# Last layer of a four-layer 2D state-space network: written order on every engine, convolution on VectorE, last epilogue in four streams

## Chip, core and metric

The kernel is one program on one core of a Trainium2 chip. A core has five engines that run side by side, each with its own queue of instructions, which it takes strictly in order: PE (TensorE, matrix products, with its weight loads shown apart as PEld), DVE (VectorE), ACT (ScalarE), POOL (GpSimd), and SP, which here only starts DMA transfers. An instruction waits on semaphores for what other engines have to deliver; what stands behind it in the same queue waits with it. The metric is the device time of one execution in microseconds. Before the change it is 21146.67 us, the median of three runs (21117.39 to 21153.36).

## What is computed

Eight images of 48 x 48 pixels and 96 channels go through four layers of the same kind, each `x = x + ss2d(groupnorm(x))`. Cut to what matters, a layer is

```python
xz = gn(x) @ in_proj_w;  xc, z = split(xz)            # 192 channels each
xc = silu(depthwise_conv3x3(xc) + conv_b)
for each of 4 directions (rows, columns, and both reversed):
    dt, B, C = split(x_dbl(xc))                       # 16 states
    delta = softplus(dt @ dt_proj_w + dt_proj_b)
    y += scan(delta, A, B, C, xc) + xc * D            # over 2304 positions
y = layernorm(sum of directions) * silu(z)
out = x + y @ out_proj_w
```

In layers 0 to 2 the scan is the recurrence `h = exp(delta*A) * h + delta*u*B`, `y = sum over states of h*C`. Layer 3, the last, writes it differently: `decay = exp(cumsum(delta*A))`, `h = decay * cumsum(delta*u*B / (decay + 1e-12))`. As the decay is a product over all earlier positions it is zero in fp32 after a while, and from there on y holds only the skip term. The kernel uses this: in the last layer it scans only the first 192 positions (`EDGE`) of each direction, records for every channel whether the decay has vanished by then (`faded`), and would run the last layer again in full under a condition at the end if one had not. That second run is in the program but isn't executed.

## The kernel before

Images go in four pairs. 192 channels of two images are laid out as three tiles of 128 partitions: channels 0 to 127 of each image, and the remaining 64 of both together. For each layer and pair there are:

- the **prologue** (L276): group norm statistics on DVE and its scaling on ACT, the input projection on PE, copied by ACT into zero-padded images (`pad`), the 3x3 depthwise convolution (`convolve`, L291), and the projection that gives dt, B and C, written to DRAM. Before the change the convolution is on PE: for each tile and each chunk of ten rows nine matmuls with a diagonal weight add up in PSUM (L301), ACT takes the sum out with the bias (L309), and a silu over the whole tile follows. A silu needs another table in ACT and is bracketed by two table loads (L259, L260);
- the **scan**, in units. For the last layer `class Edge` makes 12 groups (three tiles, two orders, two directions) of four units; a unit is four of the 16 states over 192 positions. `prepare` (L563) makes delta by softplus for a group: a product on PE (L585), four steps on ACT and two on POOL, and the last on DVE (L607), from which L609 and L611 or L614 make `dl` and `du`; `sum_up` (L839) turns `dl` into a running sum. Per unit, `decay` is four exponentials (L880) on ACT, `spread` a logarithm and an exponential (L887, L888) and four small matmuls (L893), `scan` two products and four prefix sums on DVE (L898, L899, L901) and two products with C on POOL (L905, L906), and `add_up` four matmuls into `acc` (L913), issued four units later (`LAG`). `collect` adds `acc` to y (L935) and after the last group of a tile stores y to DRAM (L939);
- the **epilogue** (L942): y comes back in 16 chunks of three rows. Per chunk: layer norm over channels by centring matmuls (L956 to L962), copy and square on ACT (L996, L997), the mean of squares on PE again, Ln and Exp (L1006, L1007), a product on DVE (L1009), scale and shift on ACT (L1012), gates from PE (L1018, L1022) through silu, a second product on DVE (L1031), and the output matmuls (L1057 to L1059 in the last layer, L1036 to L1042 in the others), a copy by ACT (L1063) and a store.

Prologue and epilogue are Python generators that yield between small steps. `run` walks over all units of all layers and pairs, in each unit issues loads for units ahead, the scan, and steps of the epilogue of the pair before (`behind`) and of the prologue of the pair to come (`ahead`), which `side_step` picks by which has made less of its way. In layers 0 to 2 the written order is kept on every engine: `keep_order` chains the instructions between two marks, and the second mark is set at the first unit of the last layer. From there on the framework's own scheduler places the instructions of each engine, from what it expects of their times. So the order that the program has in the last layer isn't the order in the source. The last pair's epilogue has nothing beside it and is issued after everything else (L1221 and after).

PSUM is given out from three pools: `ps` with two banks for everything in prologue, epilogue and softplus (`bank()`), `b` with two double banks for the spread values, `acc` with one.

Of the kernel before, what the change touches and what calls it, by code (L numbers as in the profile page):

```python
# [102 lines left out]
def ss2d_layers_kernel(ctx: ExitStack, tc: tile.TileContext, x_in, consts, weights, out):  # L103
# [172 lines left out]
    def prologue(l, p, short=False, first=False):  # L276
# [14 lines left out]
        def convolve(pad, t):  # L291
# [3 lines left out]
            u[t] = upool.tile([P, L], F32, name=f"u_{l}_{p}_{t}", tag="u")  # L295
            for c0, m in CHUNKS:
# [266 lines left out]
    def prepare(c):  # L563
# [11 lines left out]
        for z in range(0, c.m, HALF):  # L575
            m = min(HALF, c.m - z)
            at = slice(z, z + m)

            ps = bank()
# [9 lines left out]
            yield  # L589
            nc.scalar.activation(v, v, AF.Identity, bias=ly.column(t, C_DTB + k))  # L590


            e = sm1.tile([P, HALF], F32, name="e", tag="e")[:, :m]
# [348 lines left out]
    def epilogue(l, p):  # L942
# [20 lines left out]

        def three():
            return bank()[:, : 3 * EM].rearrange("p (t m) -> p t m", t=3)
# [3 lines left out]
        def load(i):  # L969
            at = slice(ECHUNKS[i][0], sum(ECHUNKS[i]))  # L970
            x = sm2.tile([DM, 2, EM], F32, name="ex", tag="ex")
            nc.sync.dma_start(x, src[:, :, at].rearrange("b c m -> c b m"))
            y = sm2.tile([P, 3, EM], F32, name="ey", tag="ey")
            nc.sync.dma_start(y, yd[:, :, at].rearrange("t p m -> p t m"))
            loaded[i] = x, y

        load(0)
        for _ in range(3):
            yield
        for i, (c0, m) in enumerate(ECHUNKS):  # L980
            at = slice(c0, c0 + m)
            x, y = loaded.pop(i)
# [5 lines left out]
            xn = sm1.tile([DM, 2, EM], F32, name="exn", tag="exn")  # L988
# [6 lines left out]
            yc = sm1.tile([P, 3, EM], F32, name="eyc", tag="eyc")  # L995
# [30 lines left out]
            if i + 1 < len(ECHUNKS):  # L1026
                load(i + 1)
# [24 lines left out]
            ps = bank()[:q, : 4 * DM].rearrange("q (h b c) -> q h b c", h=2, b=2)  # L1052
# [16 lines left out]
        del state[l, p]  # L1069
# [44 lines left out]
    def run(pairs, short):  # L1114
# [22 lines left out]

        def get_ready(k):
# [7 lines left out]
            if k == 0:  # L1146
                todo[0][1].decay(todo[0][2])
# [6 lines left out]
            for i in range(k + DECAYS if k else 1, min(k + DECAYS + 1, len(todo))):  # L1154
                todo[i][1].decay(todo[i][2])
# [12 lines left out]
        for k, ((l, p, unit), c, n) in enumerate(todo):  # L1168
            at = pairs.index((l, p))
            following = pairs[at + 1] if at + 1 < len(pairs) else None  # L1170
            if l in short and unit == 0:
                mark()
# [14 lines left out]
            if n == max(0, per - 1 - DECAYS):  # L1187
                drain(coming)
            if n == 10 and coming_to + 1 < len(chunks):
                z = chunks[coming_to + 1]  # L1190
                if (z.l, z.p) == (l, p):
                    load_dt(z)
            busy = collected()
# [5 lines left out]
            def beside():  # L1199
                step(coming)  # L1200

                for _ in range(10 if l in short else 0 if ends else 1):
                    side_step(rest) or side_step(behind, ahead)

            ends = l not in short and k >= LAG and todo[k - LAG][2] == NS - 1
            if busy and l not in short:
# [124 lines left out]
```

## Time and profile before

| | us |
|---|---|
| median of 3 runs (lowest, highest) | 21146.67 (21117.39, 21153.36) |
| the profiled execution | 21131.57 |
| its span | 21129.7 |
| first scan product of the last layer (L898) starts | 19229.4 |
| last store of y (L939) starts | 20893.1 |
| stores of the third tile of y, pairs 0 to 3 | 19617.5, 20050.2, 20486.4, 20893.1 |
| busy in the whole span: PE, DVE, ACT, POOL | 18566.6, 18834.4, 13520.6, 17984.5 |

Times in the profile are microseconds from the start of the span unless ns is written. A group line gives the source line, engine, operation, `out<-in` with shapes, the number of instructions, busy time and mean duration, and after the bar the idle time of the engine just before them with what ended it. An fp32 matmul leaves two records. Busy time of an engine merges instructions that overlap, so that it can be less than the number of instructions times their mean. A wait for several things is put down to the one that came last.

### The profile page before, as it was taken

How to read it: one execution, taken by the hardware profiler on the slowest of the kernel's cores; microseconds unless marked ns; L12 is line 12 of the kernel's file. 1: busy time of each engine (PE TensorE's matmuls, PEld its weight loads, DVE VectorE, ACT ScalarE, POOL GpSimd, SP SyncE). 2: the span in 40 equal slices, each digit the busy share in tenths (PEclk: the TensorE clock that was granted, in tenths of full speed). 3: DMA queues.
4: the chain of work that ended last, by engine and by line, in shares of the span. 5: the costliest groups of instructions: out<-in, count | busy, mean ns of one | idle time of the engine just before them, and what ended most of it. 6: DMA issues, size and time to landing. Idle time of an engine off the chain costs nothing. (4 is left out here: it accounts for less than half of the span.)

```text
span 21129.7 us, 229163 instructions
## 1 busy us (share of the span) xinstructions
PE 18566.6 (88%) x64610; PEld 9118.1 (43%) x64610; DVE 18834.4 (89%) x15938; ACT 13520.6 (64%) x23969; POOL 17984.5 (85%) x11081
## 2 busy tenths in 40 slices
PE   8988998998998998998998988998998998988886
PEld 3333444443444443443443443443443443444555
DVE  6999999999999999999999999999999999997453
ACT  5555666666666665665666666665665666667776
POOL 5999898898899899898899989898999899896442
PEclk8999999999999999999999999999999999999887
DMA  4666666676676676676676666666666666674221
GB/s 137 195 193 193 188 196 194 190 196 195 190 200 195 192 201 195 190 204 191 191 204 195 191 194 195 190 197 190 191 197 193 190 196 195 189 194 123 79 74 51
DMA packets 1707632, 3832.96 MB, mean 181 GB/s; under 512 B 238448, under 2 KB 575216, under 8 KB 1693168
## 3 DMA queue, kind: packets, MB, share of 16 engines
q1 hardware_dynamic: 1706352, 3818.21, 61.9%
q8 instruction: 521, 8.54, 0.2%
q14 instruction: 759, 6.22, 0.1%
HBM read 3665.08 MB, written 152.27 MB: 181 GB/s over the span
## 5 line engine op out<-in xcount | busy, mean ns | idle before, releaser
L804 PE MATMUL acc<-cb,cst 128*128 128x384 f32 x27648 | 10706.0, 516 | 0.0
L768 POOL TENSOR_TENSOR cb<-cb,da 128x768 f32<-128x768 f32 x5184 | 9349.5, 1813 | 1393.2 <-DVE da L759 875.6
L804 PEld LDWEIGHTS acc<-cb,cst 128*128 128x128 f32 x27648 | 5003.6, 196 | 3957.4 <-issue 1498.2
L759 DVE TENSOR_TENSOR_SCAN da<-da,carry,b 128x768 f32<-128x768 f32 x3456 | 6268.3, 1814 | 220.9 <-ACT b L726 3.7
L755 DVE TENSOR_TENSOR b<-du,b 128x768 f32<-128x768 f32 x5184 | 4912.0, 948 | 685.4 <-PE b L743 678.8
L726 ACT ACTIVATE da<-dl,a 128x768 f32<-128x768 f32 x5184 | 4770.4, 926 | 95.6 <-POOL cb L768 60.4
L743 PE MATMUL b<-brow,pick 48*128 48x512 bf16 (+3 forms) x10368 | 2652.0, 337 | 1581.8 <-DVE da L759 1239.4
L726 ACT ACTIVATE b<-dl,a 128x768 f32<-128x768 f32 x1728 | 1560.3, 903 | 2960.1 <-DVE da L759 2817.4
L698 POOL TENSOR_TENSOR bb<-bb,du 128x768 f32<-128x768 f32 x1728 | 3131.3, 1812 | 183.4 <-DMA bb<-xd 142.8
L768 POOL TENSOR_TENSOR cb<-cb,bb 128x768 f32<-128x768 f32 x1728 | 3134.0, 1814 | 161.5 <-issue 56.8
L759 DVE TENSOR_TENSOR_SCAN da<-da,b 128x768 f32<-128x768 f32 x1728 | 3030.5, 1754 | 110.2 <-ACT b L726 2.4
L743 PEld LDWEIGHTS <-pick 48*128 48x128 bf16 (+1 forms) x10368 | 669.2, 97 | 4379.9 <-DVE da L759 2363.1
L759 DVE TENSOR_TENSOR_SCAN bb<-b,carry,bb 128x768 f32<-128x768 f32 x1152 | 2069.3, 1796 | 5.9 <-ACT b L726 2.2
L301 PE MATMUL ps<-pad,diag 128*128 128x480 f32 (+1 forms) x4320 | 2015.0, 565 | 15.1 <-DVE du L611 9.6
L650 ACT COPY carry<-da 128x1 f32<-128x1 f32 x3456 | 627.1, 181 | 1086.3 <-DVE da L759 1076.4
L590 ACT ACTIVATE ps<-ps,w 128x384 f32<-128x384 f32 (+1 forms) x912 | 497.1, 545 | 1027.5 <-PE ps L585 1022.9
L301 PEld LDWEIGHTS ps<-pad,diag 128*128 128x128 f32 x4320 | 804.2, 193 | 725.2 <-issue 330.3
L603 POOL TENSOR_TENSOR lg<-lg,w 128x384 f32<-128x384 f32 (+1 forms) x912 | 892.4, 978 | 195.0 <-ACT w L601 194.8
L585 PE MATMUL ps<-dts,w 6*128 6x384 f32 (+5 forms) x2432 | 821.2, 523 | 240.6 <-DVE du L611 99.9
L759 DVE TENSOR_TENSOR_SCAN bb<-b,bb 128x768 f32<-128x768 f32 x576 | 1000.1, 1736 | 16.3 <-POOL bb L698 9.8
L604 POOL TENSOR_TENSOR lg<-lg,e 128x384 f32<-128x384 f32 (+1 forms) x912 | 889.5, 975 | 71.2
L798 PE MATMUL acc<-y,cst 128*128 128x384 f32 x1008 | 619.1, 745 | 192.2 <-ACT y L819 127.2
(141 smaller groups left out, 17243.9 us busy)
## 6 DMA issues: line engine op xcount, KB each, us to landing
cb<-xd SPq DMA_DIRECT2D x4736, 384.0 KB
cb<-xd SPq DMA_DIRECT2D x4736, 192.0 KB
bb<-xd SPq DMA_DIRECT2D x1152, 384.0 KB
bb<-xd SPq DMA_DIRECT2D x1152, 192.0 KB
yd<-y SPq DMA_DIRECT2D x48, 1152.0 KB
ey<-yd SPq DMA_DIRECT2D x256, 216.0 KB
brow<-xb SPq DMA_DIRECT2D x576, 72.0 KB
ex<-xs SPq DMA_DIRECT2D x256, 108.0 KB
```

Source lines behind the costliest of these rows:

```text
L301: nc.tensor.matmul(ps[:, :m], ly.diag[:, int(t == 2), j, :], pad[:, r0 + dy : r0 + dy + nr, dx : dx + W], start=(j == 0), stop=(j == 8),)
L585: nc.tensor.matmul(o[:, :m], ly.dtw[q0 : q0 + r, k, chans], dts[q0 : q0 + r, at], start=True, stop=True,)
L603: nc.gpsimd.tensor_sub(lg, lg, w1)
L604: nc.gpsimd.tensor_add(lg, lg, e)
L650: nc.scalar.copy(*late_act.pop(0))
L698: nc.gpsimd.tensor_mul(b, b, self.du)
L726: nc.scalar.activation(da, self.dl, AF.Exp, scale=columns_of(self.l, self.t, self.ph, self.d, n))
L743: nc.tensor.matmul(b[:, z : z + zm], w, self.brow[:k, z : z + zm], start=True, stop=True)
L755: nc.vector.tensor_mul(b, self.du, b)
L759: nc.vector.tensor_tensor_scan(way(h), way(da), way(b), start, ALU.mult, ALU.add)
L768: nc.gpsimd.tensor_mul(c, c, h)
L804: nc.tensor.matmul(self.acc[:, a, : self.m // 2], ident, c[:, a, :], start=False, stop=(n == NS - 1 and not self.turns),)
```

## The change

Only the last layer's run is edited. Everything up to a few instructions before its first unit stands in the same order on every engine as before.

1. The second mark is set after the last epilogue, so that the written order is kept on every engine throughout the last layer too. Each of its units now issues: loads and decays for units ahead, its scan, the sums of the unit four back, and then five rounds of one step of softplus for the next group (in four of the five), one step of the prologue of the pair to come and one of the epilogue of the pair before. Before there were one softplus step and ten side steps a unit. Decays are issued two units ahead of their scan, counted from the unit that is under way, where they were three ahead; dt is loaded one group ahead of its softplus, where softplus itself used to load it.
2. In pairs 1 to 3 of the last layer the convolution is done by VectorE: nine instructions over a whole tile of 128 x 2304, one per tap, with the bias in the first. Pair 0 still has it on PE, in the layer before.
3. Softplus of the last layer moves its argument from PSUM into the free half of the tile `e` in SBUF, so that the bank is free after one read.
4. The last epilogue is split in four streams, each with every fourth chunk, stepped in turns and started three turns apart. Streams 2 and 3 take their PSUM tiles from the pool of the spread values. Streams 1 to 3 keep their four SBUF tiles in one buffer of another pool, and load a chunk when they begin it, not one ahead.

```diff
@@ convolve, at its start
+            if l == NLAYER - 1 and p > 0:
+                v = u[t].rearrange("p (r w) -> p r w", w=W)
+                for j in range(9):
+                    dy, dx = divmod(j, 3)
+                    z = pad[:, dy : dy + H, dx : dx + W]
+                    tap = ly.column(t, C_CONVW + j)
+                    if j == 0:
+                        nc.vector.tensor_scalar(
+                            v, z, tap, ly.column(t, C_CONVB), ALU.mult, ALU.add
+                        )
+                    else:
+                        nc.vector.scalar_tensor_tensor(v, z, tap, v, ALU.mult, ALU.add)
+                    yield
+                silu(u[t], u[t])
+                yield
+                return
@@ prepare
-            yield
-            nc.scalar.activation(v, v, AF.Identity, bias=ly.column(t, C_DTB + k))
-            e = sm1.tile([P, HALF], F32, name="e", tag="e")[:, :m]
+            e = sm1.tile([P, HALF], F32, name="e", tag="e")
+            if c.m == EDGE:
+                v = e[:, EDGE : 2 * EDGE]
+            else:
+                yield
+            nc.scalar.activation(v, ps[:, :m], AF.Identity, bias=ly.column(t, C_DTB + k))
+            e = e[:, :m]
@@ epilogue
-    def epilogue(l, p):
+    def epilogue(l, p, part=0, parts=1):
+        def own_bank():
+            return bank() if part < 2 else pb.tile([P, 2 * BANK], F32, name="b", tag="b")
...
         def load(i):
+            if part:
+                w = tmp.tile([P, 10 * EM], F32, name="ew", tag="tmp")
+                x, xn = (...)                      # x, exn, y, eyc all in w
...
-        load(0)
+        mine_of = range(part, len(ECHUNKS), parts)
+        load(part)
         for _ in range(3):
             yield
-        for i, (c0, m) in enumerate(ECHUNKS):
+        for i in mine_of:
+            c0, m = ECHUNKS[i]
+            if i not in loaded:
+                load(i)
...
-            if i + 1 < len(ECHUNKS):
-                load(i + 1)
+            if not part and i + parts < len(ECHUNKS):
+                load(i + parts)
@@ run, in each unit
-            if l in short and unit == 0:
-                mark()
...
-            if n == max(0, per - 1 - DECAYS):
+            if n == per - 1 - (1 if l in short else DECAYS):
                 drain(coming)
-            if n == 10 and coming_to + 1 < len(chunks):
+            if n == (0 if l in short else 10) and coming_to + 1 < len(chunks):
...
+            if l in short:
+                get_ready(k + 1)
+                c.scan(n)
+                collected()
+                catch_up()
+                if k >= LAG:
+                    (bl, bp, _), b, bn = todo[k - LAG]
+                    b.add_up(bn)
+                    if todo[k - LAG + 1][0][:2] != (bl, bp):
+                        done = bl, bp
+                if n == 0:
+                    while ahead.held and behind.held:
+                        side_step(behind)
+                for i in range(5):
+                    if i < 4:
+                        step(coming)
+                    side_step(ahead)
+                    side_step(behind)
+                continue
@@ run, at its end
-        drain(epilogue(*pairs[-1]))
+        streams = [epilogue(*pairs[-1], part, 4) for part in range(4)]
+        turn = 0
+        while streams:
+            streams = [g for i, g in enumerate(streams) if turn < 9 and turn < 3 * i or next(g, g) is not g]
+            turn += 1
+        mark()
```

## The prediction

> **What bounds the kernel now.** I read the page's slices first, then busy time by stretches, then the groups and waits of the last layer, then a timeline. Slices (busy tenths, 40 equal parts of the span):
>
> ```profile
> PE   8988998998998998998998988998998998988886
> ...
> DVE  6999999999999999999999999999999999997453
> ...
> PEclk8999999999999999999999999999999999999887
> ```
>
> VectorE (DVE) is full for 36 slices, the first three layers, and drops in the last four. The built order of every engine is unchanged until a few instructions before the last layer, so only the stretch from its first unit (19229 us) to the end counts: 1900 us of 21129.7. Busy time in its four pairs and its last epilogue (columns: stretch, length, busy us and records of PE, PE weight load, DVE, ACT, POOL, clock, DMA share, GB/s):
>
> ```profile
> 19229.00:19600.00 371.00, 328.87 (x1648) 218.93 (x1647) 206.97 (x367) 300.23 (x558) 177.84 (x119) 0.93 0.30 84
> 19600.00:20035.00 435.00, 366.38 (x1948) 252.71 (x1948) 225.36 (x393) 346.09 (x645) 191.44 (x135) 0.89 0.27 75
> 20035.00:20471.00 436.00, 365.81 (x1982) 252.73 (x1982) 224.77 (x392) 342.96 (x641) 191.43 (x134) 0.89 0.27 75
> 20471.00:20882.00 411.00, 273.40 (x1778) 223.93 (x1779) 220.25 (x386) 320.67 (x607) 185.20 (x121) 0.80 0.25 70
> 20893.00:21125.00 232.00, 153.65 (x1026) 130.80 (x1026) 19.52 (x34) 118.26 (x190) 0.00 (x0) 0.74 0.14 36
> ```
>
> In the first three pairs PE leads (84 to 89%) with ScalarE (ACT) close (79 to 81%); in the fourth, without a prologue, ACT leads (78%). In the last epilogue nothing does (PE 66%, ACT 51%): it is a chain. Its waits:
>
> ```profile
> DVE eyc L1009 <- ACT ps L1007: 171.8, 16, 16.3
> ACT eyc L996 <- PE ps L962: 50.5, 16, 22.5
> ...
> ACT eo L1063 <- PE ps L1059: 36.7, 16, 3.2
> ACT ps L1006 <- PE ps L962: 34.8, 16, 3.6
> ```
>
> Sixteen waits of each kind, one for each of 16 row chunks: 13.7 us a chunk (L1006 starts at 20936.40 and at 20950.23 on the chain). Groups of 19300 to 20850 (busy, mean ns, then idle before):
>
> ```profile
> L301 PE MATMUL ps<-pad,diag 128*128 128x480 f32 x632 | 265.7, 574 | 4.9 <-DVE eyc L1009 4.9
> L880 ACT ACTIVATE da<-dl,a 128x192 f32<-128x192 f32 x687 | 262.3, 443 | 26.0 <-DVE dl L839 25.8
> ...
> L899 DVE TENSOR_TENSOR b<-rq,b 128x768 f32<-128x768 f32 x171 | 162.6, 956 | 220.7 <-ACT rq L888 219.6
> ```
>
> The convolution is PE's largest group; VectorE waits for ACT. Last, a VectorE instruction with both inputs in SBUF, beside a GpSimd (POOL) product:
>
> ```profile
> 20095.12 1.81 POOL L906 TENSOR_TENSOR cb<-cb,rq 128x768 f32<-128x768 f32 x1 [1.38 <-DVE rq L901]
> 20095.21 2.13 DVE L839 TENSOR_TENSOR_SCAN dl<-ones,dl 128x192 f32<-128x192 f32 x1
> ```
>
> L839 has a median of 0.549 us; here it ends 0.4 us after POOL's product.
>
> [...] a pair of output passes takes 0.17 us between convolutions and 0.32 us in the last epilogue (clock 0.74). [...]
>
> **The change part by part.** Unit costs, from the groups and timelines. A unit (four states of 192 positions) is on ACT four decays, Ln and Exp, 4x0.443+0.925+0.834 = 3.53, back to back some 3.15 (six decays together take 2.18 us, not 2.66); DVE two products and four scans, 3.8; POOL 2x1.81 = 3.6; PE 0.65 for the spread and 1.7 for the sums. Softplus adds 2.25 of ACT to every fourth unit. One chunk of an epilogue is 118.26/16 = 7.4 of ACT, and the chain of 13.7.
>
> *Order.* Before, a scheduler places the instructions; now the written order holds on each engine: per unit the scan part, then five rounds of softplus, one prologue step and one epilogue step. Twelve epilogue steps make a chunk, so a chunk takes 2.4 units. Units 0 to 3 and five at the end have no side work: 9x4.3 = 39 (the last 16 units of before took 62 us, 3.9 each). With the epilogue alone: ACT 3.15+0.55+7.4x5/12 = 6.8. I walked the queues by hand through one cycle of 12 units (five chunks). Where a unit ends behind the silu, the next scan part hides the output passes; where it does not, as in the fifth unit, ACT is through its scan part at 3.15 and the silu at 6.2, whose result L1031 has multiplied by 5.6; the passes then last until 9.45 and the copy until 9.9, after 3.2 us of waiting. That happens in two chunks of five; a wait of 2.0 for the second mean (between L997 and L1006) in two others; shorter ones everywhere. Some 3.7 a chunk, 1.5 a unit: 8.3.
>
> *Convolution.* Removed per pair: 135 matmuls, 270 records of 0.41 us dense (18 take 7.4) = 111 us of PE, and 15 evictions of 0.64 = 9.6 of ACT. Added: 27 VectorE taps of 128x2304. The nearest row, L607, rises from 0.366 at 192 to 0.54 us at 384 elements, which gives 2.3; [...] I take 2.5[...]. That is 67 us a pair. Taps have two SBUF inputs, so each can stand behind a POOL product: 0 to 1.81 us. About two products fall in two units of taps: 3.6 a tile. Taps stand in two or three units per tile (in the second pair units 10 and 11, 18 to 20, 32 and 33). DVE then needs 2x3.8+22.5+3.6 = 34 for two units against 16.6; ACT can run ahead about one unit before its output copy and the tile's silu wait: net +13 a tile. Queued behind the taps are the epilogue's two products (L1009, L1031), and behind those ACT's next steps and the next scan.
>
> *Sum of a middle pair.* 17 units with the two images' prologue: ACT 17x6.8+20 copies of 0.5+6 for normalising+two silus of 4.65 = 141; waits 17x1.5 = 26; two convolutions 26: 193. Eleven with the epilogue alone: 91. Two with the third convolution: 43 (34 of DVE, 4 for softplus products and sums between the taps, the silu's 4.65 behind the last). Nine with projections: 8.3 and some 0.5 of copies each, 79. With 39: 445, against 435 and 436 before. The first pair's epilogue has 12 output records for 24: 20 less, 425, against 371. The last pair has no prologue: 39x8.4+39 = 367, against 411. Together 1682 against 1653: +29.
>
> *PE clock.* [...] the walk uses the slow 3.85 for outputs. Fast (2.0) would save up to 1.8 x16 a pair where ACT waits for it, some 12.
>
> *Softplus in SBUF* frees a PSUM buffer; its two products now can wait for POOL (0 to 1.8 each, twelve groups a pair). Nothing on ACT, as it is prepared a group ahead; without that cover, up to 20 a pair. *Loads.* Rows for C still go out three units ahead; earlier decay and dt moves only fill ACT's queue. The SP queue keeps written order, so a store that waits for L1063 holds the loads behind it, by less than a unit of the three: nothing. The 6.65 us store of y before the epilogue's first load stays in both.
>
> *Last epilogue.* Four streams share engines in turns. Bound: ACT 7.4 a chunk, PE 6.3 at full clock (outputs 2.0, the two means 1.6 each, gates 1.1), 153.65/16 = 9.6 at the clock of before. I take 8.4: streams 1 to 3 load without prefetch, 12 loads of 2.8 us landing, each issued about a turn early (0 to 34 together; I take 12). 16x8.4+7 for first store and load+14 until all streams run and drain+6 = 161, against 232: -71. Bounds: 145 and 205.
>
> Net +29-71 = -42: a span of 21088. The profiled execution took 21131.57, 15 under the median 21146.67 (runs spread 36); carried to the median: 21105. About 42 us (0.2%) is what a measurement can tell.
>
> **Rivals.** *Slower: the taps wait for POOL.* If every tap stands behind a product, 27x1.81 = 49 a pair instead of 11, three pairs +114: net +72, 21220. For it: L839's 2.13 and 3.65 for two; POOL has 3.6 a unit. Against: only two products a unit exist, unless waiting POOL and DVE alternate. It decides from 28 more a pair.
>
> *Faster: engines slip over units.* ACT stays 82% busy, as the walk has it without taps: busy (346 less 10 and some table loads, 332) gives 405 for each middle pair, by the same step about 360 and 375 for the first and last: 1545, a gain of 108. I keep 70 of it, since the taps' 13 a tile cannot all go; with -71 that is -141: 21005. For it: PE's 84 to 89% falls to some 60. Against: in-order waits of L1012 and L1063 behind taps.
>
> *No difference: the streams hold each other.* Two PSUM buffers for each two streams, and late loads: the last epilogue gains 25, not 71: net about 0, 21147.
>
> **How the numbers follow.** Forecast 0.45 (0.25 beyond -0.2%, 0.20 within; own range 21045 to 21165), faster rival 0.17, slower 0.30, no difference 0.08 (0.06 within, 0.02 slower). So faster 0.42, same 0.26, slower 0.32. The range leaves out half of the faster case and a third of the slower, 0.085 and 0.10: 21000 to 21235.
>
> **What would show it.** Right: taps near 2.5 us with some up to 4.3; pairs of 445, 367 last; the last epilogue near 161 with clock above 0.8; PE below 75% in the pairs. Wrong: middle pairs under 415 or over 470; taps of 4 us on average; a last epilogue above 200 with PE waiting for ey loads.

## The result, and the profile after

In what follows, before and after stand for the kernel before and the kernel after the change. After takes 21400.03 us (median of 4 runs, 21379.71 to 21419.24), before beside it 21150.01 (21117.39 to 21154.85). The ratio is 1.012, with a 95% interval of 1.0108 to 1.0132: about 250 us slower, outside the predicted range and beyond the slower rival as well. The slices of the page of after, in the same form as before:

```profile
PE   8988988988988988988988988988989988986666
...
DVE  6999999999999999999999999999999999996664
...
PEclk9999999999999999999999999999999999996777
```

The last layer now stands out on every engine at once: TensorE is at six tenths where it was at eight or nine, and its granted clock falls to seven tenths. VectorE rises from 4 or 5 tenths to 6. No engine is full, so the time went to waiting. Busy time in the four pairs and in the last epilogue (columns: stretch, its length, busy us and records of TensorE, its weight loads, VectorE, ScalarE, GpSimd, the clock, DMA share, GB/s):

```profile
19246.00:19757.00 511.00, 312.89 (x1500) 235.83 (x1500) 335.41 (x412) 339.29 (x626) 205.34 (x133) 0.70 0.23 65
19757.00:20276.00 519.00, 318.56 (x1712) 247.07 (x1712) 339.41 (x421) 338.00 (x625) 209.20 (x134) 0.70 0.23 63
20276.00:20795.00 519.00, 318.59 (x1712) 246.14 (x1712) 338.58 (x420) 337.25 (x622) 209.13 (x134) 0.71 0.23 63
20795.00:21204.00 409.00, 277.44 (x1638) 235.62 (x1638) 253.36 (x379) 296.23 (x554) 186.33 (x118) 0.75 0.24 70
21217.00:21417.00 200.00, 138.18 (x1026) 124.08 (x1026) 19.48 (x33) 116.55 (x192) 0.00 (x0) 0.79 0.16 43
```

In the second pair the three busiest engines have 339, 338 and 319 us of work in 519: 65% at most. ScalarE's work hardly moved (338 against 346). For the comparison of kernels I use one pair of marks throughout: a pair lasts from the first scan product of its first unit (L920, before L898) to the next pair's, the last pair to the last store of y, and the last epilogue from there to the end.

| us | pair 0 | pair 1 | pair 2 | pair 3 | four pairs | last epilogue |
|---|---|---|---|---|---|---|
| before | 413.1 | 437.4 | 435.7 | 377.5 | 1664 | 237 |
| after | 513.5 | 518.4 | 519.2 | 417.7 | 1969 | 200 |

The pairs lost 305 us, the epilogue gained 36. Layers 0 to 2 came 19 us later in this profiled execution (first L920 at 19248.1, against 19229.4); their order is unchanged, and the first scan product of the last layer starts anywhere from 19203 to 19248 us in the runs below. 305 - 36 + 19 is the 288 us between the two spans. So the pairs and the last epilogue are compared from here on, and not the totals alone.

VectorE's groups in the last layer of after (line, operation, `out<-in` and shapes, number, busy us and mean ns, idle before and its releaser):

```profile
L308 DVE SCALAR_TENSOR_TENSOR u<-pad,w,u 128x2304 f32<-128x2304 f32 x72 | 225.3, 3129 | 1.8
...
L861 DVE TENSOR_TENSOR_SCAN dl<-ones,dl 128x192 f32<-128x192 f32 x47 | 59.0, 1256 | 45.1 <-ACT dl L631 45.1
L629 DVE SCALAR_TENSOR_TENSOR e<-e,lg 128x192 f32<-128x192 f32 x47 | 52.9, 1125 | 81.8 <-POOL lg L626 81.8
L636 DVE TENSOR_TENSOR du<-e,u 128x192 f32<-128x192 f32 x24 | 43.1, 1798 | 0.7
L633 DVE TENSOR_TENSOR du<-e,u 128x192 f32<-128x192 f32 x23 | 39.5, 1717 | 0.5
```

A tap (L308) takes 3.13 us on the mean, with a smallest of 2.59 and a median of 2.62. With the first taps (L304, 2.38) the convolution is 247 us of VectorE, 82 a pair. The softplus's end grew too: L607 had 0.366 us before and is L629 with 1.125 now, and its two products went from 0.35 and 0.46 to 1.72 and 1.80. Together with the running sum (L861) these are 194.5 us, where the same four groups of before, from its first unit to its last store of y, are 73.5. The waits of after from 19200 us on (engine, its tile and line, who released it and where: us in total, times, longest):

```profile
POOL cb L928 <- DVE rq L923: 610.7, 130, 16.4
POOL lg L625 <- ACT w L623: 280.8, 47, 12.6
ACT e L612 <- PE ps L603: 277.3, 47, 22.5
DVE eyc L1053 <- ACT ps L1051: 265.1, 57, 18.3
...
DVE eyc L1075 <- ACT ps L259: 195.4, 44, 9.9
PE acc L935 <- DVE y L957: 193.5, 26, 20.3
PE ps L1102 <- DVE eyc L1075: 162.9, 33, 9.8
ACT eo L1107 <- PE ps L1103: 129.3, 38, 6.3
```

GpSimd, the least busy of the four, waits for VectorE and ScalarE; ScalarE waits for TensorE, VectorE for ScalarE, TensorE for VectorE. No engine is the one that all others wait for. A stretch of the timeline in the last pair shows one turn of this ring (start, length, instruction, idle time before it and who ended it):

```profile
20867.13 2.20 ACT L946 ACTIVATE y<-u,dsum 128x2304 f32<-128x2304 f32 x1
20869.36 0.35 DVE L957 TENSOR_TENSOR y<-y,acc 128x192 f32<-128x192 f32 x1 [6.65 <-ACT y L946]
...
20869.87 2.90 PE L935 MATMUL acc<-cb,cst 128*128 128x192 f32 x8 [3.34 <-DVE y L957]
...
20872.69 1.00 PE L603 MATMUL ps<-dts,w 6*128 6x192 f32 x2
...
20873.73 0.42 ACT L612 ACTIVATE e<-ps,w 128x192 f32<-128x192 f32 x1 [4.40 <-PE ps L603]
```

ScalarE writes the skip term of y; VectorE has stood 6.65 us for it, to collect a finished group; only then may TensorE put the next group's first sum (L935) into the one accumulator; behind these sums stands the softplus's product L603, for which ScalarE has meanwhile waited 4.40 us. My walk had none of these steps: it didn't ask when `acc` comes free.

### The profile page after: what moved, and what is told of

The parts are those of the page before. It is cut to its first block, busy times and chain, and to the rows that moved or that the text cites. A ratio compares the mean times of both kernels' runs of the same rounds, so it can differ in the third digit from the quotient of the medians.

```text
span 21417.4 us, 227251 instructions
## 1 busy us (share of the span) xinstructions
PE 18469.9 (86%) x63800; PEld 9133.3 (43%) x63800; DVE 19214.0 (90%) x16019; ACT 13506.1 (63%) x23910; POOL 18044.0 (84%) x11081
## 4 chain that ended last, share of the span: by engine, by line
DVE 43%; PE 27%; ACT 12%; issue 10%; DMA 6%; POOL 2%; SPq 1%; DVEq 0%; POOLq 0%; ACTq 0%
DVE da L781 21%; DVE b L777 12%; PE acc L826 12%; DVE bb L781 4%; DMA cb<-xd 3%; PE b L765 3%; PE ps L318 3%; PE acc L820 2%; PE ps L603 2%; ACT da L748 2%; ACT b L748 2%; DVE ps L629 1%; DMA brow<-xb 1%; POOL cb L790 1%; ACT y L841 1%
## 5 line engine op out<-in xcount | busy, mean ns | idle before, releaser
L318 PE MATMUL ps<-pad,diag 128*128 128x480 f32 (+1 forms) x3510 | 1695.7, 569 | 9.6 <-DVE du L633 9.6
L612 ACT ACTIVATE ps<-ps,w 128x384 f32<-128x384 f32 x864 | 478.4, 554 | 1024.0 <-PE ps L603 1019.6
L928 POOL TENSOR_TENSOR cb<-cb,rq 128x768 f32<-128x768 f32 x192 | 364.0, 1896 | 810.4 <-DVE rq L923 610.7
L603 PE MATMUL ps<-dts,w 6*128 6x384 f32 (+5 forms) x2432 | 831.3, 529 | 217.6 <-DVE du L633 79.9
L318 PEld LDWEIGHTS ps<-pad,diag 128*128 128x128 f32 x3510 | 654.4, 194 | 572.8 <-issue 207.0
```

The costliest lines, as they stand in the source:

```text
L318: nc.tensor.matmul(ps[:, :m], ly.diag[:, int(t == 2), j, :], pad[:, r0 + dy : r0 + dy + nr, dx : dx + W], start=(j == 0), stop=(j == 8),)
L603: nc.tensor.matmul(o[:, :m], ly.dtw[q0 : q0 + r, k, chans], dts[q0 : q0 + r, at], start=True, stop=True,)
```

## The experiments

I began with three causes that the profile suggests, each as a theory of its own: **A**, the single accumulator (the ring above); **B**, the lock between VectorE and GpSimd over the softplus in SBUF (a VectorE instruction with two operands in SBUF and a GpSimd product hold each other up: L839 in the forecast's timeline takes 2.13 us for a median of 0.549, and in after GpSimd's products, with a median of 1.81 us, last up to 4.13 beside taps); **C**, the taps. The rival to all three is that the order itself costs. In what follows, before's median in the same comparison lies between 21127 and 21141 us.

**1. Two accumulators.**

```diff
-                self.acc = pacc.tile([P, 2 * BANK], F32, name="acc", tag="acc")
+                if "acc" not in place:
+                    place["acc"] = pacc.tile([P, 2 * BANK], F32, name="acc", tag="acc")
+                self.acc = place["acc"][:, BANK * (groups.index((self.t, self.ph, self.d)) % 2) :]
```

> The kernel after, but the groups of the last layer add up by turns in two accumulators, the two banks of the same PSUM tile, so that a group's first sum no longer waits until VectorE has collected the group before. Nothing else is changed. Theory A, the accumulator holds the loop (first sum L935 waits for the collecting L957, the softplus matmul stands behind it on TensorE, and ScalarE waits for that): 100 to 180 us less than after, so 21220 to 21300, and the waits of L935 for VectorE, 193.5 us over 26 in after, gone. Theory B, the lock between VectorE and GpSimd over the softplus sets the period: within 30 us of after. Theory C, the convolution's taps on VectorE set it: within 30 us of after.

Measured 21390.56 us (1.0127, 1.011 to 1.0144), pairs of 514, 518, 519 and 418. But the first sum still waits for the collecting, 193.4 us over 26, as in after. The edit did not take the wait away, so it tests nothing. That the two banks of one tile count as one thing for the synchronisation is my guess at the reason; the new wait in the next experiment, between two banks of the same tile, fits it.

**2. The softplus's argument in a free PSUM bank.**

```diff
-                v = e[:, EDGE : 2 * EDGE]
+                v = place["acc"][:, BANK : BANK + EDGE] if "acc" in place else e[:, EDGE : 2 * EDGE]
```

> The kernel after, but the argument of the softplus goes to the unused second bank of the accumulator instead of SBUF, for all groups but the first of the layer, so that VectorE's three operations of it read one operand from PSUM and two no longer come from SBUF. Theory B, the lock with GpSimd: VectorE's sum of the three operations and the running sum falls from 194.5 us to about 75 in the 48 groups, and the time by 90 to 130 us, to 21270 to 21310. Theory A, the accumulator: 20 to 40 us less at most, since VectorE only comes a little earlier to the collecting. Theory C: the same 20 to 40.

Measured 21397.24 us (1.0132, 1.0115 to 1.0149). The lock is gone from the operations that now have an operand in PSUM, as VectorE's groups show:

```profile
L629 DVE SCALAR_TENSOR_TENSOR acc<-acc,lg 128x192 f32<-128x192 f32 x46 | 16.5, 360 | 188.5 <-PE acc L937 132.2 <-POOL lg L626 23.8 <-ACT da L902 23.0
...
L636 DVE TENSOR_TENSOR du<-acc,u 128x192 f32<-128x192 f32 x24 | 11.3, 473 | 31.9 <-ACT dl L631 31.9
L633 DVE TENSOR_TENSOR du<-acc,u 128x192 f32<-128x192 f32 x22 | 7.8, 355 | 22.8 <-ACT dl L631 22.8
```

0.36 us in the place of 1.125, and the sum of all four groups falls from 194.5 to 89 us. The time stands still, since a new wait of 132 us for TensorE's sums into the same tile came in. So B's mechanism is shown, but not its price: the run took one wait and brought another.

**3. The convolution on TensorE, order kept.** In `convolve` the taps make way for nine matmuls and an eviction a step:

```diff
-                        nc.vector.scalar_tensor_tensor(v, z, tap, v, ALU.mult, ALU.add)
...
+                    for j in range(9):
+                        nc.tensor.matmul(ps[:, :m], ly.diag[:, int(t == 2), j, :], ...)
+                    yield True
```

> The kernel after, but the convolution of the last layer's later images runs on TensorE again, nine matmuls and one eviction a step, in the place of the taps in the order. Theory C, the taps: VectorE loses 247 us, the three pairs with a prologue lose 60 to 90 each, so 21130 to 21220. Theory A: the taps are 82 us of a pair on an engine that the collecting waits for, 20 to 40 a pair come back, 21280 to 21340. Theory B: the same as A. The granted clock of TensorE in those pairs, 0.70 in after, should rise above 0.80 in each case.

Measured 21474.36 us (1.0163, 1.0146 to 1.018), with pairs of 540, 547, 553 and 413: the first three slower than after by some 30 each. The loss stays without the taps, so C falls as its cause. Of two kernels with the order kept, the one with taps is the better; what the taps alone cost isn't shown, as the matmuls that take their place stand in the order too. The clock of TensorE rose to 0.81 in the second pair, as all three theories said, with 404 us of work in 547.

**4. The same kernel, placed by the scheduler.**

```diff
             if l in short:
+                if unit == 0:
+                    mark()
                 get_ready(k + 1)
```

> The kernel after, but the last layer's instructions are placed by the scheduler as before, from the same written order, taps, softplus and streams. If the fixed order itself is what costs (each queue stands behind the first instruction that waits): 150 to 250 us less than after, 21150 to 21250. If the places of the data cost (the softplus in SBUF, the one accumulator, the taps on VectorE): less than 60 us less, 21340 or more.

Measured 20963.88 us, a ratio of 0.9921 (0.9905 to 0.9938): 436 us less than after, and faster than before. Taps, softplus, one accumulator, units' turns and streams are all still there. Its stretches, first the four pairs, then the last epilogue:

```profile
19247.00:19648.00 401.00, 291.10 (x1524) 220.97 (x1522) 302.83 (x414) 328.01 (x623) 222.79 (x134) 0.78 0.30 86
19648.00:20053.00 405.00, 290.04 (x1716) 226.41 (x1716) 305.34 (x419) 333.13 (x631) 225.66 (x135) 0.79 0.28 80
20053.00:20469.00 416.00, 299.42 (x1713) 232.59 (x1712) 302.44 (x414) 332.64 (x629) 224.43 (x131) 0.76 0.27 77
20469.00:20832.00 363.00, 252.13 (x1638) 210.61 (x1638) 230.80 (x383) 297.16 (x570) 189.28 (x120) 0.82 0.27 76
20832.00:20966.00 134.00, 108.45 (x1026) 94.97 (x1026) 19.38 (x33) 110.10 (x184) 0.00 (x0) 0.95 0.22 59
```

The same work with the same engine time (ScalarE 333 us in the second pair, 338 in after) takes 405 us where it took 519: ScalarE is now 82% busy. The pairs cost 1584 us, 385 less than in after, and the last epilogue 134, 66 less. The wait of the first sum for the collecting does not come up among the longest any more. So the loss lies in the order that was kept. Each engine has one sequence in either kernel: TensorE's 1712 records, VectorE's 419 and ScalarE's 622 of after's second pair come back line for line in its third, and so do the 1982, 392 and 641 of before, where the scheduler placed them. The scheduler's queues are simply other ones than the source's. "Kept" below always means this one written order. No run tries another written order, so whether a better one would do as well as the scheduler's stays open.

**5. One engine's order kept.** These runs keep the order on TensorE alone, ScalarE alone, VectorE alone:

```diff
-    def keep_order(a, b):
+    def keep_order(a, b, engines=ENGINES):
...
     keep_order(*marks[:2])
+    keep_order(*marks[1:3], ENGINES[:1])     # or [2:3], or [1:2]
```

> The kernel after, with the written order of the last layer kept on TensorE alone; the scheduler places the other four engines' instructions. With all five kept it takes 21400, with none 20964. If the first sum of a group, which waits for the accumulator with the softplus matmul behind it, is what stops the loop, TensorE's order alone brings most of the 436 us: 21250 or more. If it is another engine's order, less than 100 of them: below 21065.

> The same with the order kept on ScalarE alone. ScalarE carries most of a unit's other steps (decay, spread, softplus, silu, evictions), so a wait at its head holds everything: if that is the cause, 21200 or more. If TensorE's order is the cause: below 21065. In the last epilogue the streams' written turns should show on ScalarE first: 160 to 200 us there against 134 in the scheduled one.

> The same with the order kept on VectorE alone, where the taps, the softplus and the collecting stand between the scans. If a tap or a softplus step at the head of the queue holds the scans: 21150 or more. If the order of TensorE or ScalarE is the cause: below 21065.

Measured 20976.51 us (0.9924, 0.9907 to 0.994), 20997.71 (0.9931, 0.9914 to 0.9947) and 20969.62 (0.9925, 0.9908 to 0.9941). The expectations speak of the whole layer, but a mark is set at the first unit of every pair, so the order was kept in the first pair only. There the pair takes 427.8, 457.9 and 431.4 us, against 401.0 with none kept and 513.5 with all five: TensorE's order costs 27 us, ScalarE's 57, VectorE's 30. None alone brings the 113. These prices are rough: the second pair, where nothing is kept in these runs or in the scheduled kernel, takes 405 to 417 us.

**6. The streams alone in the kernel before**, with `epilogue` and its streams from after, and everything placed by the scheduler:

```diff
-        drain(epilogue(*pairs[-1]))
+        streams = [epilogue(*pairs[-1], part, 4) for part in range(4)]
...
```

> The kernel before, with only the last epilogue in four streams, all placed by the scheduler. The scheduled kernel with all the edits has an epilogue of 134 us, before has 236. If the streams carry the gain of the scheduled kernel: 21010 to 21050, 80 to 110 less than before. If they owe it to the rest (the taps and the softplus in SBUF, 80 us over the four pairs): the same epilogue gain, and the pairs as before, so that these two add up to the 163 us between the scheduled kernel and before. If they help only together with the rest: less than 50.

Measured 21029.69 us, 0.9951 (0.9934 to 0.9968). The last epilogue is 136 us, against 237, and the pairs are as before (417, 437, 435, 382). So of the 163 us by which the scheduled kernel beats before, the streams bring 100.

**7. Collecting ahead of the scan**, the order kept, as another test of A:

```diff
-                c.scan(n)
                 collected()
+                c.scan(n)
```

> The kernel after, all five orders kept, but in each unit of the last layer the collecting of the finished group stands ahead of the unit's scan on VectorE and not behind it. Theory A, the accumulator holds the loop: the 193.5 us over 26 that the first sum waits for VectorE fall below 60, and the time by 60 to 150, to 21250 to 21340. Theory D, the orders together cost because each unit's work lies unevenly over the engines and every unit lasts as long as its busiest: the wait moves to another line, the time within 40 us of after.

Measured 21339.18 us (1.0094, 1.0077 to 1.0111), 61 less than after, which is A's smallest gain; A's other sign, a wait below 60 us, did not come. The pairs are 500, 504, 504 and 410. Its waits:

```profile
ACT e L612 <- PE ps L603: 199.5, 40, 18.7
...
PE acc L935 <- DVE y L957: 138.9, 19, 16.5
...
DVE y L957 <- ACT y L946: 109.9, 12, 12.9
```

The first sum still waits 139 us, because VectorE itself now waits longer for ScalarE's skip term (110 us, 54 in after). A is a part of the loss, some 15 us a pair by this way of shortening it. It is not the whole.

**8. One engine freed.** The order of the last layer kept on four engines, or on three:

```diff
+    keep_order(marks[1], marks[5], ENGINES[:2] + ENGINES[3:])   # ScalarE free
+    keep_order(marks[1], marks[5], ENGINES[:1] + ENGINES[2:])   # VectorE free
+    keep_order(marks[1], marks[5], ENGINES[1:])                 # TensorE free
+    keep_order(marks[1], marks[5], ENGINES[:3])                 # GpSimd and DMA queue free
+    keep_order(marks[1], marks[5], ENGINES[:2])                 # TensorE and VectorE kept
```

> The kernel after, with the written order kept on four engines in the last layer's four pairs and all of ScalarE's instructions placed by the scheduler (the last epilogue is placed by it on all engines; the order of layers 0 to 2 is kept as ever). Each engine's order alone, kept in the first pair only, cost 27 us (TensorE), 57 (ScalarE) and 30 (VectorE) there, where all five cost 113. If these add up engine by engine, the pairs lose 45 to 55 us each against the fully scheduled 401, 405, 416, and ScalarE's share is gone: 21100 to 21170 in all. If ScalarE's order is the one that couples the others, the loss is gone with it: below 21040. If the other four hold each other without it: above 21200.

> The kernel after, with the order of the last layer kept on four engines and VectorE placed by the scheduler. In after VectorE stands at the head of its queue for epilogue steps (L1053 266 us, L1075 195 us) and for the collecting while scans that could run stand behind. If VectorE's fixed order is what couples the engines, the pairs fall from 518 to 400 to 440: 20980 to 21130. If any four hold each other as with ScalarE free (505): 21250 or more.

> The same with TensorE free: the sums, with the softplus matmul and the prologue's and epilogue's matmuls behind them, may pass one another. If TensorE's fixed order couples the engines: pairs of 400 to 440, 20980 to 21130. If any four hold each other: pairs of about 500, 21250 or more.

> The order kept on TensorE, VectorE and ScalarE together, GpSimd and the DMA queue placed by the scheduler. If the three compute engines suffice to hold each other: pairs of 490 to 520, 21300 or more. If GpSimd's products standing behind its softplus steps (L625 waits 281 us for ScalarE in after) or the loads in the DMA queue are part of the hold: pairs below 470, below 21220.

> The order of the last layer kept on TensorE and VectorE together, the other three engines placed by the scheduler. Fully scheduled, a pair takes 401 to 416; in the first pair, TensorE's order alone gave 428 and VectorE's alone 431; with three engines kept (TensorE, VectorE, ScalarE) 507 to 512. If the cost comes as soon as two engines cannot slip against each other: pairs of 470 or more, 21150 or more. If their costs only add: pairs of 440 to 465, about 21100.

In all five the order was kept in the last epilogue as well. The expectation of the first says otherwise, and is wrong in that.

| order kept on | median us | ratio to before, interval | pair 0 | pair 1 | pair 2 | pair 3 | last epilogue |
|---|---|---|---|---|---|---|---|
| all five (after) | 21400.03 | 1.0108 to 1.0132 | 513.5 | 518.4 | 519.2 | 417.7 | 200 |
| all but ScalarE | 21311.48 | 1.007 to 1.0103 | 500.9 | 504.6 | 504.9 | 387.4 | 193 |
| all but VectorE | 21329.27 | 1.0074 to 1.0108 | 487.7 | 493.7 | 494.5 | 420.5 | 200 |
| all but TensorE | 21234.15 | 1.003 to 1.0064 | 490.7 | 494.3 | 491.6 | 383.2 | 150 |
| TensorE, VectorE, ScalarE | 21327.49 | 1.0077 to 1.011 | 507.1 | 511.6 | 511.9 | 417.8 | 167 |
| TensorE, VectorE | 21187.56 | 1.0013 to 1.0034 | 475.1 | 476.1 | 474.7 | 365.8 | 171 |
| none | 20963.88 | 0.9905 to 0.9938 | 401.0 | 404.5 | 415.9 | 362.8 | 134 |

Read by their expectations, the rest hold each other whichever of TensorE, VectorE and ScalarE is freed (with TensorE free the total, 21234, falls just short of the 21250 named, since the last epilogue gains 50 there), three are enough, and two cost somewhat more than the sum of their single prices: 74 us in the first pair for 27 + 30, which is 17 more with some 12 us of scatter in such prices. Freeing one of the three gives a middle pair back 14 to 28 of some 110 us, and freeing GpSimd with the DMA queue 7. So in the pairs with a prologue no engine's order is the cause by itself; what costs there is that the written order stands on several engines at once. The last pair, without prologue and taps, is different: of the 55 us that it loses, 34 come back with TensorE free and 30 with ScalarE free, none with VectorE free, and with TensorE and VectorE alone kept it loses 3 (366 against 363).

How several fixed queues lose can be read from the units. I cut each engine's queue at its own instruction of each unit (first scan product, second step of the reciprocal on ScalarE, first spread matmul, first C product), took of the four busy times in each unit the largest, and added these over the 48 units of the second pair. If all engines went through the units in step, none working into its neighbour unit, and nothing else was waited for, a pair would last about that long:

| second pair | busiest engine's work | sum of units' largest | measured |
|---|---|---|---|
| after | 342 | 455 | 518.4 |
| TensorE, VectorE, ScalarE kept | 337 | 453 | 511.6 |
| all but ScalarE kept | 350 | 498 | 504.6 |
| all but VectorE kept | 337 | 445 | 493.7 |
| all but TensorE kept | 340 | 496 | 494.3 |
| TensorE, VectorE kept | 344 | 468 | 476.1 |
| none kept | 337 | 465 | 404.5 |

The scheduled kernel is 60 us below that sum, so its engines run ahead of each other over unit bounds. After is 64 us above: in the sum its engines gain nothing by slipping past each other, and waits between them come on top. With two or more orders kept the second pair is at most 2 us below its sum; with one kept, the first pair is below it by 5 (TensorE), 17 (ScalarE) and 66 (VectorE). The sum alone does not order the kernels, since the scheduled one has a larger sum than after, and it depends on the cuts: with TensorE's cut one unit later after has 465. It is a reading of how the time goes, and no proof. The chain of waits gives an example. This piece of after's chain, from its second pair (start, length, instruction), goes from ScalarE's queue into VectorE's at an epilogue step, and then through three taps that stand there back to back, 9.3 us in all, and a product of the epilogue (L1075); the next unit's scan (L920) stands behind them.

```profile
19865.42 0.52 ACT ps L1051
19865.94 0.02 issue
19865.97 0.60 DVE eyc L1053
19866.57 2.54 DVE u L308
19869.11 0.03 issue
19869.13 4.05 DVE u L308
19873.18 0.02 issue
19873.21 2.62 DVE u L308
19875.83 0.51 DVE eyc L1075
19876.34 0.88 DVE b L920
```

**9. What the parts are worth under the scheduler.** From the scheduled kernel: the convolution back on TensorE; the softplus's argument back in its own bank; both; the softplus back and only one of three tiles with taps.

```diff
-            if l == NLAYER - 1 and p > 0:                 # (removed: convolution on TensorE)
...
-                v = e[:, EDGE : 2 * EDGE]
+            yield
+            nc.scalar.activation(v, v, AF.Identity, bias=ly.column(t, C_DTB + k))
...
+            if l == NLAYER - 1 and p > 0 and t == 1:      # (in the last: one tile)
```

> The scheduled kernel with all edits (20964), but the later images' convolutions on TensorE again. If the taps carry the gain of its pairs over before (80 us in four pairs; TensorE's convolution is 75 of a pair's 438 us in before's chain of work): 30 to 90 us more, 20995 to 21055, and the granted clock of TensorE in the pairs changes with it. If they don't: within 20 us.

> The scheduled kernel with all edits (20964), but the softplus's argument stays in its PSUM bank as before. VectorE's operations of it are short again (0.37 and 0.35 us against 1.13 and 1.72), but each softplus holds one of the two banks over six steps. If the bank is dearer: 20 to 60 us more than 20964. If the lock with GpSimd is dearer: 20 to 60 us less, 20905 to 20945.

> The scheduled kernel with both the softplus in its PSUM bank and the convolutions on TensorE, so that of the change only the turns of the units and the four streams stand. Undone alone, the softplus gave 24 us and the convolution 17. If they add up: 20910 to 20935. If each pays because it takes load off VectorE where the other one put it: 20930 to 20950. Against before with the streams alone (21030) the difference is what the turns are worth under the scheduler: 80 to 120 us.

> The scheduled kernel with the softplus in its PSUM bank and only one of a pair's three convolutions (channel tile 1) as taps on VectorE. In the pair's 405 us TensorE is busy for 394 with all three convolutions on it, ScalarE for 341 and VectorE for 227; one convolution moved takes some 27 us from TensorE and gives VectorE about 27. If TensorE's load is what sets a pair there: pairs of 380 to 395, 20840 to 20890. If the chain through all engines does: within 15 of the 20918 with none moved.

| scheduled | median us | ratio to before, interval | pairs 0 to 3 |
|---|---|---|---|
| all edits | 20963.88 | 0.9905 to 0.9938 | 401, 405, 416, 363 |
| convolution on TensorE | 20947.00 | 0.9896 to 0.9929 | 396, 406, 406, 366 |
| softplus in PSUM | 20939.71 | 0.9892 to 0.9925 | 402, 416, 408, 355 |
| both | 20918.03 | 0.9885 to 0.9918 | 405, 405, 406, 355 |
| softplus in PSUM, one tile with taps | 20911.82 | 0.9875 to 0.9908 | 399, 401, 401, 352 |

The intervals overlap: taps and softplus in SBUF make no difference that these runs can tell. With both undone the median is 46 us lower; but of the 52 us between the two profiled executions 39 lie ahead of the last layer, and the pairs and the last epilogue differ by 13. The turns of the units do make one. With both undone only the streams and the turns (with the decays and loads that go with them) are left of the change, and 0.9901 against 0.9951 for the streams alone is 0.5%, with intervals apart; the pairs take 1572 us against 1671. One tile moved takes a pair from 405 to 401 us, not to 380 to 395, so TensorE's load alone is not the bound of the scheduled pairs either. (Its 394 us in the expectation were too many: the stretch of that pair has 364 us of TensorE's work.) The last kernel takes 1.1% less than before and some 2.3% less than after.

## Why the prediction was wrong

**Order.** This is the step that failed. It priced the written order at 1.5 us of waits a unit, from one cycle of queues walked by hand, and only the epilogue's own waits were in that. The 445 us of a middle pair, some 56 of them such waits (37 units of 1.5), became 518 to 519, the first pair's 425 became 511 to 514, the last pair's 367 became 409 to 418. (The 371 and 411 that I set against the first and last came from stretches that end ahead of the pair and begin ahead of it; by the marks used here before has 413 and 378, and 1664 in all four for my 1653, so that this changes little in the sum.) The last pair has neither prologue nor taps, so some 55 us are lost there by the order with the epilogue alone: with no order kept it takes 363, close to my 367. The two middle pairs lie 114 and 103 above their scheduled times, 405 and 416. The walk left out three handoffs that the trace shows: the accumulator (193.5 us of waiting), the softplus's product behind it (277.3), and the softplus's last steps on VectorE behind GpSimd. Easing one at a time gave 3 to 61 us, and in both runs another wait grew (132 us for TensorE's sums, 110 for the skip term). Outside the convolutions I also took a unit's length from ScalarE's queue; in the second pair ScalarE has the most work in 15 of the 48 units, VectorE in 18, TensorE in 13. These largest alone come to 455, so that my 445 is near them and has hardly anything for the waits between the engines on top.

**Convolution.** The mechanism was right and the size nearly so. 2.5 us a tap was the forecast: L607's two lengths gave 2.3, and no trace had shown the rest. 2.6 is the plain length: the smallest tap is 2.591 us and the median 2.619. Waiting behind GpSimd was put at 11 us a pair (3.6 a tile); 72 taps x (3.129 - 2.6) over three pairs are 12.7. The whole is 82 us a pair for 67 + 11. With the order kept, the kernel without the taps was even the slower one.

**Softplus in SBUF.** I had put it at nothing for ScalarE, and at up to 20 us a pair if being prepared a group ahead did not cover it. Its operations on VectorE take 121 us more in the layer (194.5 against 73.5), 30 a pair: all 47 of its products and 23 of 47 L629 start beside a GpSimd product and are long. The second operand in SBUF makes the difference: with one operand in PSUM (experiment 2) the same L629 takes 0.360 us and not 1.125, and L607 of before, which reads PSUM, takes at most 0.367 beside a GpSimd product as it does alone. The cover holds under the scheduler, where the form of the softplus can't be told in the time. With the order kept its price is open, since the run that took away the lock put another wait there.

**PE clock.** Up to 12 us a pair were kept back for a faster clock. It went the other way: 0.70 in the middle pairs (0.89 before), and the same 1536 records of the sums took 401 us in the layer, where before has 352. In the second pairs the clock went with TensorE's busy share: 0.70 at 61% (after), 0.79 at 72% (scheduled), 0.81 at 74% (experiment 3), 0.89 at 84% (before) and 0.91 at 90% (scheduled, with softplus and convolution both undone). I had reckoned with a changed clock in the output passes alone. In the scheduled kernel the clock is 0.76 to 0.79 in the pairs with a prologue, with shorter pairs. So the low clock goes with the waiting; how much it adds to it wasn't separated.

**Last epilogue.** 161 forecast, 200 measured, gain 36 and not 71. The bounds, 145 and 205, held. The streams themselves can do 134 (scheduled), below my lower bound. Two orders hold them most: with TensorE free the same streams take 150, and with GpSimd and the DMA queue free 167, which is the DMA queue's doing, since GpSimd has no instruction there. With ScalarE or VectorE free they take 193 and 200. In after the DMA queue stands 161 us for results that it has to store, with loads behind them in its order, and 35 us when it is free; I had counted 12 us for late loads. TensorE ran at 0.79 of its clock, where it has 0.95 in the scheduled epilogue, and its 1026 records took 138 us and not 108. My 8.4 us a chunk took a middle clock without an account of who waits.

**Rivals.** The slower one named the wrong mechanism: taps in wait for GpSimd. The time passed its 21220, but such waiting was 12.7 us a pair and not its 49. "Engines slip over units" described what the same instructions do under the scheduler: 405 and 416 us for a middle pair where it said 405, with ScalarE 82% busy as it said, and 20964 in all for its 21005. What I had not seen is that this written order leaves little room for the slip. My case against it named taps ahead of two instructions, and the forecast gave the rest of the order away as nearly free. "The streams hold each other" was the nearest for the last epilogue, with a gain of 25 where 36 were measured: its late loads fit what the freed DMA queue gave back, but its two PSUM buffers were not what held, since the scheduled streams have the same ones and take 134. The signs named for a wrong forecast, middle pairs over 470, came.

## What to carry to other kernels

What stands behind a waiting instruction waits with it (in the ring above TensorE stood 3.34 us for the collecting, with the softplus's product behind the sums), so writing the order for several engines by hand means that every producer must be early in its queue and every consumer late in its own, all at once. Before one fixes it, each buffer with a single copy and each handoff in a unit has to be walked, not only the busiest engine. Afterwards, a pair that lasts longer than the sum of its units' largest engine times is a sign that the engines don't run ahead of each other. If such a change loses, let the scheduler place the same source first: here that edit of two lines separated a gain of 0.8% from a loss of 1.2%, while freeing one engine, or easing one wait, left most of the loss in place.

## What the runs showed that I had not expected

- No single wait decided. Beside GpSimd's own, four waits of 190 to 280 us each stand in after's list. Of the 436 us that the order costs, collecting earlier gave back 61, the softplus without its lock 3, and taking the taps away cost 74 more.
- VectorE's operation with two SBUF operands stands behind GpSimd's whole product, again and again. In after these three take 1.95, 1.85 and 2.15 us in alternation with products of 1.8 us, for plain lengths of 0.37, 0.35 and 0.55:

```profile
20266.20 1.82 POOL L927 TENSOR_TENSOR cb<-cb,da 128x768 f32<-128x768 f32 x1
20266.27 1.95 DVE L629 SCALAR_TENSOR_TENSOR e<-e,lg 128x192 f32<-128x192 f32 x1 [3.97 <-POOL lg L626]
...
20268.09 1.81 POOL L928 TENSOR_TENSOR cb<-cb,rq 128x768 f32<-128x768 f32 x1
...
20268.26 1.85 DVE L633 TENSOR_TENSOR du<-e,u 128x192 f32<-128x192 f32 x1
...
20269.85 1.92 POOL L927 TENSOR_TENSOR cb<-cb,da 128x768 f32<-128x768 f32 x1
20270.04 2.15 DVE L861 TENSOR_TENSOR_SCAN dl<-ones,dl 128x192 f32<-128x192 f32 x1
```

- Four independent streams over two pools of PSUM took an epilogue of 237 us to 134, with the granted clock up from 0.74 to 0.95 and TensorE's busy time down from 154 to 108 us for the same 1026 records.
